# A graph network's edge strips: preparing edges in six steps, one-hots a group ahead, one multiplication for three

## The chip, the cores and the metric

The kernel runs on one core of a Trainium2 chip. Its engines are TensorE (PE; its weight loads are listed as PEld), VectorE (DVE), ScalarE (ACT), GpSimd (POOL) and the queue that issues most transfers (SP). The metric is the device time of one launch in microseconds, median of several runs. Times within the profiled execution are counted from the start of its span.

## The reference

Four graph layers over 6250 nodes with 128 features and 206250 edges, sorted by target `dst`. Each layer works on `h = relu(layernorm(x))` and is added to `x`:

```python
# layer 0: weighted sum over the edges, two products
neighbor = segment_sum(edge_weight[:, None] * h[src], dst)
x += leaky_relu(neighbor @ W1.T + b1 + (h * neighbor) @ W2.T + b2, 0.2)
# layer 1: mean over the edges, gelu, a norm over all nodes
agg = segment_sum(h[src], dst) / max(deg, 1)
f = gelu(agg @ Wl.T + bl + h @ Wr.T);  x += graph_norm(f) + h
# layer 2: mean of the cliques' rows at the other end
x += mean(x_clique[dst], by=src) @ W.T + b
# layer 3: a gated unit on the summed messages
x += gru(segment_sum((h @ W_in.T + b_in) @ W_msg, dst), ...) @ W_out.T + b_out
```

## The kernel before

The kernel does not gather rows. It turns the edges into dense matrices: for each block of 128 target nodes, how often each source node occurs (`cnt`, kept in device memory for layers 1 to 3) and the sum of its edge weights (`edge_w`, used at once by layer 0). The 6250 nodes are 49 blocks; a **strip** is two blocks, 256 target nodes, and there are 25 strips (the last has one block). All of this is done in the first part of `fast`, up to line 829; behind it `dense` (line 838) reads the matrices back for layers 1 to 3, and that part is not touched.

A strip goes through these hands:

- `prepare(k)` finds the edges of every target node. DVE counts in a sample of `dst` (`junk`, line 628) where a node's edges begin; POOL fetches a `line` of 128 edges there (635, by an indirect transfer, the helper `fetch` at line 620); DVE counts within it (`less`, `c`, `off`). For each of two halves POOL then fetches 64 entries of `dst` (655); DVE marks those of the node (`same`, 657), moves `off` on by their number and marks the others (661); POOL fetches `src` and the weights. DVE splits `src` into a block and a place in it (666 to 670, `vals` 1 and 0), POOL splits the weight into three parts (672, `vals` 2 to 4). PE transposes the five (676) and ACT copies them to `by_edge` (678). Its working tiles have one buffer each (`once`), `vals` and `by_edge` two.
- `count` takes 32 target nodes at a time, a **group**; a strip has eight. For a group DVE makes the one-hots: `s_hot` (696) and `k_hot`, first the block alone (698), then times each of the three weight parts (700). PE multiplies them in 96 small matmuls, 24 to each of four tiles `pK` (713), and ACT copies each `pK` to `cnt` (727) and `edge_w` (728). The one-hots have two buffers, `pK` three, `cnt` two. After four groups a `cnt` is complete: SP writes it to `cnt_d` (736), and for the first 25 blocks turns it in seven pieces (741, `tt` with three buffers) and stores these too (742).
- `layer0(k)` runs one strip later, a step of six products `pL` (749) behind each group, then the copy `agg` (754), a transpose (757) and `inter` (759).
- `finish0` runs one strip later still, in three steps: the products with W1 and W2 (768, 769), bias and leaky relu (`full`), the norm of the result (`norm`, called at 779: statistics on DVE, `f_std` on ACT at 558, `f_rstd` and `f_shift` on DVE, the relu on ACT at 565), stores of `u_d` and `h_d`; then the transposes of `h1` (786); then the product with Wr (793), `fs` (795) and its store.
- `norms` makes `h0` from `x` in the first strips.

The source interleaves them by generators: after each group of `count` one step of the layer before and one of its end is asked for. `prepare` of the next strip is asked for whole at the strip's beginning, except for the transposes, which are asked for after group 4. A scheduler takes this order as a priority only: it places each instruction on its engine when its inputs and a free buffer are there by its own reckoning, so an engine's sequence can differ from the source's. Once placed, each engine works its sequence in order.

Of the kernel before, what the change touches and what calls it, by code (L numbers as in the profile page):

```python
# [16 lines left out]
P = 128  # L17
# [468 lines left out]
def fast(ctx: ExitStack, tc: tile.TileContext, a: dict, out: bass.AP, flag: bass.AP):  # L486
# [62 lines left out]
    def norm(xs, hs, nb):  # L549
# [3 lines left out]
        for j in range(nb):  # L553
# [27 lines left out]
    with ExitStack() as bx:  # L581
# [22 lines left out]
        def norms():  # L604

            for g, nb in GROUPS:
                xs = xpool.tile([P, GB, D], F32, name="xs")
                load_x(xs, g, nb)
                norm(xs, h0[:, g : g + nb, :], nb)
                if g // GB % 2:  # L610
                    yield
# [11 lines left out]
        def prepare(k):  # L623
# [11 lines left out]
            fetch(line, "dst", at_i)  # L635
            less = once.tile([P, P], BF16, name="less")
# [12 lines left out]
            for h in range(WN):  # L649
# [5 lines left out]
                fetch(dst[:, half], "dst", off_i)  # L655
                here = deg[:, k, h : h + 1]
# [7 lines left out]
                fetch(wgt[:, half], "edge_weight", off_i)  # L664
            sb = once.tile([P, P], I32, name="sb")
# [15 lines left out]
        def count(k, nb, by_edge, edge_w):  # L681


            mats = []
            for t0 in range(0, nb * P // WN, TW):
                tq = TW // TI

                def at(i, n):
                    v = by_edge[:, i, t0 : t0 + TW].rearrange("p (q o t) -> p q o t", o=1, t=TI)
                    return v.to_broadcast([P, tq, n, TI])  # L690

                def count_up(n):
                    return iota[:, None, :n, :].to_broadcast([P, tq, n, TI])

                s_hot = hot.tile([P, tq, P, TI], BF16, name="s_hot")
                nc.vector.tensor_tensor(s_hot, count_up(P), at(0, P), op=ALU.is_equal)  # L696
                k_hot = hot.tile([P, 4, tq, NB, TI], BF16, name="k_hot")
                nc.vector.tensor_tensor(k_hot[:, 0], count_up(NB), at(1, NB), op=ALU.is_equal)  # L698
                for i in range(1, 4):
                    nc.vector.tensor_tensor(k_hot[:, i], k_hot[:, 0], at(1 + i, NB), op=ALU.mult)  # L700
                for q in range(0, TW, PW):

                    pk = psum.tile([P, WN, 512], F32, name="pK", bufs=3)
                    for i in range(PW):
                        (u, t), o = divmod(q + i, TI), 2 * NB * i
                        for j in (0, 2, 3):
                            for h in range(WN):
                                r = slice(h * H, (h + 1) * H)
                                if j:
                                    to, rhs = slice(o + NB, o + 2 * NB), k_hot[r, j, u, :, t]  # L710
                                else:
                                    to, rhs = slice(o, o + 2 * NB), k_hot[r, :2, u, :, t]
                                nc.tensor.matmul(pk[:, h, to], s_hot[r, u, :, t], rhs, start=j == 0,  # L713
                                                 stop=True, skip_group_check=True)
                    n0 = (t0 + q) * WN
                    nn = PW * WN
                    if n0 % P == 0:
                        mats.append(cnts.tile([P, NB, P], BF16, name="cnt"))

                    def by_block(half):  # L720
                        v = pk[:, :, : 2 * PW * NB].rearrange("p h (i c b) -> p c b i h", c=2, b=NB)
                        return v[:, half]

                    def to_nodes(m):
                        return m.rearrange("p b (i h) -> p b i h", h=WN)

                    nc.scalar.copy(to_nodes(mats[n0 // P][:, :, n0 % P : n0 % P + nn]), by_block(0))  # L727
                    nc.scalar.copy(to_nodes(edge_w[:, :, n0 : n0 + nn]), by_block(1))  # L728
                yield
                n0 = (t0 + TW) * WN  # L730
                if n0 % P:
                    continue
                j = n0 // P - 1
                g = k * SB + j
                c, i = CHUNK_OF[g]
                nc.sync.dma_start(cnt_d[c, :, i, :], flat(mats[j]))
                if g >= NQB:
                    continue
                for q in range(0, NB, 7):
                    tt = turned.tile([P, 7, P], BF16, name="tt")  # L740
# [79 lines left out]
        for _ in ends.pop():  # L820
            pass
# [315 lines left out]
```

## Time and profile before

| what | value |
| --- | --- |
| median of 3 runs | 2179.38 us (2178.58 to 2182.17) |
| the profiled execution | 2177.09 us, span 2175.3 us, 60376 instructions |
| TensorE clock granted, mean | 0.962 |
| first matmul of the strips (L713) | at 53.0 us |
| strips 0 to 24 | 53.0 to about 1224 us |
| dense layers behind them | about 1224 to 2175 us |
| DVE one-hots L696, L698, L700 | 239.3, 114.4 and 307.9 us busy, for 196 groups |
| PE L713 and L749 | 420.8 and 590.0 us busy |
| ACT L727 and L728 | 407.5 and 415.1 us busy |

The busy times of PE are modelled and overlap, so they are read with the distances between groups in the timeline. A line number names the line of the kernel that issued an instruction; where a helper issues it, it is the helper's (POOL's fetches are all L620, and are told apart by their tiles). The bracket behind an instruction in the timeline is the idle time of its engine just before it and what ended it.

### The profile page before, as it was taken

The numbers are of one execution on the slowest core, as the hardware profiler recorded it, in microseconds if no ns is written. First come the engines' busy times: TensorE is split into PE (matmuls) and PEld (weight loads), VectorE is DVE, ScalarE is ACT, GpSimd is POOL, SyncE is SP. The second block draws the span as 40 slices with busy tenths as digits, with TensorE's granted clock in tenths as the row PEclk, the third lists the DMA queues.
The fourth block names the chain that finished last, engine by engine and source line by source line (L and its number), as shares of the span: only waits on it lengthen the run. The fifth ranks groups of instructions, "written<-read, shape, count | busy, mean of one in ns | idle before, by whom it ended". The sixth has DMA issues, their size and how long they took to land. (4 is left out here: it accounts for less than half of the span.)

```text
span 2175.3 us, 60376 instructions
## 1 busy us (share of the span) xinstructions
PE 1910.5 (88%) x25624; PEld 1564.8 (72%) x25624; DVE 1411.9 (65%) x3349; ACT 1174.2 (54%) x2692; POOL 348.3 (16%) x377
## 2 busy tenths in 40 slices
PE   0579988889898999998999679999878899999998
PEld 0557777777787888777888558878756667777775
DVE  6887767767676776776775458677776554443443
ACT  1745656555555666566666146566545555443443
POOL 4531211222212122111100020000231110000000
PEclk9989999999999999999999789999989999999999
DMA  2579999999998222223122698688755778776773
GB/s 63 154 177 229 216 213 212 231 204 217 220 229 194 86 105 93 90 85 105 73 101 103 197 265 278 214 283 270 228 164 174 231 236 262 239 229 197 237 239 128
DMA packets 423787, 406.32 MB, mean 187 GB/s; under 512 B 191216, under 2 KB 414307, under 8 KB 417235
## 3 DMA queue, kind: packets, MB, share of 16 engines
q1 hardware_dynamic: 414883, 394.35, 64.1%
q0 software_dynamic: 5600, 6.56, 1.3%
q8 instruction: 203, 3.33, 0.6%
q10 hardware_dynamic: 3024, 1.45, 0.3%
q14 instruction: 77, 0.63, 0.1%
HBM read 227.26 MB, written 134.89 MB: 166 GB/s over the span
## 5 line engine op out<-in xcount | busy, mean ns | idle before, releaser
L727 ACT CAST cnt<-pK 128x392 bf16<-128x392 f32 x784 | 407.5, 520 | 342.1 <-PE pK L713 289.5
L749 PE MATMUL pL<-edge_w,h 128*128 128x256 f32 (+1 forms) x2450 | 590.0, 392 | 1.1 <-issue 0.8
L713 PE MATMUL pK<-k_hot,s_hot 64*128 64x49 bf16 (+1 forms) x18816 | 420.8, 195 | 126.4 <-ACT edge_w L728 66.0
L713 PEld LDWEIGHTS <-s_hot 64*128 64x128 bf16 x18816 | 371.0, 96 | 197.2 <-issue 119.8
L749 PEld LDWEIGHTS pL<-edge_w,h 128*128 128x128 f32 x2450 | 456.9, 196 | 66.2 <-issue 1.2
L728 ACT COPY edge_w<-pK 128x392 f32<-128x392 f32 x784 | 415.1, 529 | 0.0
L870 PE MATMUL acc<-some,parts 128*128 128x512 f32 (+1 forms) x1456 | 369.4, 395 | 31.3 <-DVE some L865 20.6
L870 PEld LDWEIGHTS acc<-some,parts 128*128 128x128 f32 x1456 | 269.6, 192 | 95.7 <-DVE some L865 24.4
L696 DVE TENSOR_TENSOR s_hot<-iota,by_edge 128x2048 bf16<-128x2048 bf16 x196 | 239.3, 1221 | 133.7 <-PE pK L713 129.2
L700 DVE TENSOR_TENSOR k_hot<-k_hot,by_edge 128x784 bf16<-128x784 bf16 x588 | 307.9, 576 | 5.2
L859 ACT CAST others<-ring 128x1536 fp32r<-128x1536 bf16 (+3 forms) x156 | 192.4, 1233 | 198.3 <-PE acc L870 132.2
L858 DVE CAST some<-ring 128x2048 fp32r<-128x2048 bf16 (+3 forms) x156 | 165.7, 1063 | 177.8 <-PE acc L870 151.6
L870 PE MATMUL acc<-others,parts 128*128 128x512 f32 (+1 forms) x1092 | 277.7, 388 | 0.0
L865 DVE TENSOR_SCALAR_CACHE_REDUCE some<-ring 128x512 fp32r<-128x512 bf16 (+1 forms) x364 | 216.6, 651 | 62.7 <-PE acc L870 43.1
L870 PEld LDWEIGHTS acc<-others,parts 128*128 128x128 f32 x1092 | 202.5, 191 | 42.5 <-issue 0.5
L868 ACT ACTIVATE others<-ring 128x512 fp32r<-128x512 bf16 (+1 forms) x273 | 162.3, 597 | 113.1 <-issue 59.6
L870 PE MATMUL acc<-some,q_parts 128*128 128x512 f32 (+1 forms) x390 | 111.5, 412 | 30.6 <-DVE some L858 30.6
L698 DVE TENSOR_TENSOR k_hot<-iota,by_edge 128x784 bf16<-128x784 bf16 x196 | 114.4, 583 | 0.0
L870 PEld LDWEIGHTS acc<-some,q_parts 128*128 128x128 f32 x390 | 71.2, 196 | 51.4 <-DVE some L858 35.5
L657 DVE TENSOR_SCALAR_CACHE_REDUCE same<-dst,node 128x64 bf16<-128x64 int32 x50 | 13.9, 277 | 137.7 <-DMA dst<-in_dst,off_i 137.7
L780 POOL TENSOR_TENSOR xs<-xs,h 128x256 f32<-128x256 f32 (+1 forms) x25 | 27.3, 1090 | 466.3 <-ACT h L565 466.3
L870 PE MATMUL acc<-others,q_parts 128*128 128x512 f32 (+1 forms) x260 | 78.3, 409 | 0.0
(155 smaller groups left out, 1520.6 us busy)
## 6 DMA issues: line engine op xcount, KB each, us to landing
ring<-cnt_d SPq DMA_DIRECT2D x168, 896.0 KB
cnt_d<-cnt SPq DMA_DIRECT2D x49, 1568.0 KB
cntT_d<-tt SPq DMA_DIRECT2D x175, 224.0 KB
ring<-cntT_d SPq DMA_DIRECT2D x60, 640.0 KB
ring<-cnt_d SPq DMA_DIRECT2D x14, 224.0 KB
xs<-in_x SPq DMA_DIRECT2D x24, 128.0 KB
xs<-in_x SPq DMA_DIRECT2D x12, 256.0 KB
h_d<-h SPq DMA_DIRECT2D x24, 128.0 KB
```

Source lines behind the costliest of these rows:

```text
L696: nc.vector.tensor_tensor(s_hot, count_up(P), at(0, P), op=ALU.is_equal)
L698: nc.vector.tensor_tensor(k_hot[:, 0], count_up(NB), at(1, NB), op=ALU.is_equal)
L700: nc.vector.tensor_tensor(k_hot[:, i], k_hot[:, 0], at(1 + i, NB), op=ALU.mult)
L713: nc.tensor.matmul(pk[:, h, to], s_hot[r, u, :, t], rhs, start=j == 0, stop=True, skip_group_check=True)
L727: nc.scalar.copy(to_nodes(mats[n0 // P][:, :, n0 % P : n0 % P + nn]), by_block(0))
L728: nc.scalar.copy(to_nodes(edge_w[:, :, n0 : n0 + nn]), by_block(1))
L749: nc.tensor.matmul(pl[:, :w], h0[:, s, :], edge_w[:, s, :w], start=s == 0, stop=s == NB - 1)
L858: nc.vector.tensor_copy(some[:, :dve, :nb], t[:, :dve])
L859: nc.scalar.copy(others[:, : step - dve, :nb], t[:, dve:])
L865: nc.vector.tensor_scalar(rhs, t[:, i], 1.0, None, op0=ALU.mult, op1=ALU.add, accum_out=total)
L868: nc.scalar.activation(rhs, t[:, i], AF.Copy, accum_out=total)
L870: nc.tensor.matmul(acc[:, :w], parts[:, q + i, j, :], rhs, start=q + i + j == 0, stop=q + i + j == last)
```

## The change

Five things. `prepare` gets yields after the fetch of `line`, after each fetch of `dst`, after the last fetches and after the weights' split, and its transposes are the sixth step; the main loop asks for one step behind each group. The one-hots become a function of their own, `one_hots`, called for the next group (or the next strip's first) before `count` is called for this one. `norm` gets three yields, so `finish0` has six steps, and the loop asks for it before the layer's step instead of after. `by_edge` becomes two tiles in another order of axes, copied by two instructions, so that one multiplication writes all three weighted parts of `k_hot`. The stores of a finished `cnt` are a function `store`, called at the same place.

```diff
@@ norm
         nc.vector.tensor_scalar(std[:, :nb], mv[:, :nb, 1], EPS, None, op0=ALU.add)
+        yield
         nc.scalar.activation(std[:, :nb], std[:, :nb], AF.Sqrt)
+        yield
 ...
         nc.vector.scalar_tensor_tensor(shift[:, :nb], mv[:, :nb, 0], -1.0, rstd[:, :nb],
                                        op0=ALU.mult, op1=ALU.mult)
+        yield
@@ prepare
             fetch(line, "dst", at_i)
+            yield
 ...
                 fetch(dst[:, half], "dst", off_i)
+                yield
 ...
                 fetch(wgt[:, half], "edge_weight", off_i)
+            yield
 ...
-            by_edge = pay.tile([P, 5, P], BF16, name="by_edge")
-            nc.scalar.copy(by_edge, pv)
+            keys = pay.tile([P, P // TI, 2, TI], BF16, name="keys")
+            parts = pay.tile([P, P // TI, 3, TI], BF16, name="by_edge")
+            for t, i in ((keys, 0), (parts, 2)):
+                to = pv[:, i : i + t.shape[2], :].rearrange("p i (q t) -> p q i t", t=TI)
+                nc.scalar.copy(t, to)
+            by_edge = keys, parts
             yield by_edge
@@ count, now one_hots and count
+        def one_hots(by_edge, t0):
+            of = slice(t0 // TI, t0 // TI + tq)
+            keys, parts = (t[:, of, :, None, :] for t in by_edge)
 ...
+            s_hot = hot.tile([P, tq, P, TI], BF16, name="s_hot")
+            nc.vector.tensor_tensor(s_hot, count_up(P), at(0, P), op=ALU.is_equal)
-                k_hot = hot.tile([P, 4, tq, NB, TI], BF16, name="k_hot")
-                nc.vector.tensor_tensor(k_hot[:, 0], count_up(NB), at(1, NB), op=ALU.is_equal)
-                for i in range(1, 4):
-                    nc.vector.tensor_tensor(k_hot[:, i], k_hot[:, 0], at(1 + i, NB), op=ALU.mult)
+            k_hot = hot.tile([P, tq, 4, NB, TI], BF16, name="k_hot")
+            nc.vector.tensor_tensor(k_hot[:, :, 0], count_up(NB), at(1, NB), op=ALU.is_equal)
+            nc.vector.tensor_tensor(k_hot[:, :, 1:], k_hot[:, :, :1].to_broadcast([P, tq, 3, NB, TI]),
+                                    parts.to_broadcast([P, tq, 3, NB, TI]), op=ALU.mult)
+            return s_hot, k_hot
+        def count(t0, hots, mats, edge_w):
+            s_hot, k_hot = hots
 ...
+        def store(g, mat):
 ...
@@ finish0
-            norm(xs, h1, nb)
+            yield from norm(xs, h1, nb)
@@ the main loop
-        edges, before, ends = prepare(0), norms(), []
-        next(edges)
-        by_edge = next(edges)
+        for by_edge in prepare(0):
+            pass
+        before, ends, hots = norms(), [], one_hots(by_edge, 0)
         for k, nb in STRIPS:
             edges = prepare(k + 1) if k + 1 < NS else iter(())
-            next(edges, None)
             edge_w = edge.tile([P, NB, SW], F32, name="edge_w")
-            end = ends.pop() if ends else iter(())
-            turned_edges = None
-            for i, _ in enumerate(count(k, nb, by_edge, edge_w)):
-                next(before, None)
-                next(end, None)
-                if i == 4:
-                    turned_edges = next(edges, None)
-            by_edge = turned_edges
+            end, mats, following = ends.pop() if ends else iter(()), [], None
+            for t0 in range(0, nb * P // WN, TW):
+                now, t1 = hots, t0 + TW
+                if t1 * WN < nb * P:
+                    hots = one_hots(by_edge, t1)
+                elif following:
+                    hots = one_hots(following, 0)
+                count(t0, now, mats, edge_w)
+                next(end, None)
+                next(before, None)
+                following = next(edges, None) or following
+                if t1 * WN % P == 0:
+                    store(k * SB + len(mats) - 1, mats[-1])
+            by_edge = following
             for _ in chain(before, end):
                 pass
             before = layer0(k, nb, edge_w)
-        for _ in chain(ends.pop(), before):
-            pass
-        for _ in ends.pop():
-            pass
+        end = ends.pop()
+        for _ in before:
+            next(end, None)
+        for _ in chain(end, ends.pop()):
+            pass
```

The other two callers of `norm` run through its steps at once.

More of the change, by code (lines that the diff above doesn't have):

```diff
@@ L608, in norms @@
                 load_x(xs, g, nb)
-                norm(xs, h0[:, g : g + nb, :], nb)
+                for _ in norm(xs, h0[:, g : g + nb, :], nb):
+                    pass
                 if g // GB % 2:
@@ L676, in prepare @@
                 nc.tensor.transpose(pv[:, i, :], vals[:, i, :], identh)
-            by_edge = pay.tile([P, 5, P], BF16, name="by_edge")
-            nc.scalar.copy(by_edge, pv)
-            yield by_edge
[L681 to L696, printed above, removed]
-                k_hot = hot.tile([P, 4, tq, NB, TI], BF16, name="k_hot")
-                nc.vector.tensor_tensor(k_hot[:, 0], count_up(NB), at(1, NB), op=ALU.is_equal)
-                for i in range(1, 4):
[L700 to L740, printed above, removed]
-                    nc.sync.dma_start_transpose(tt, flat(mats[j][:, q : q + 7, :]))
-                    nc.sync.dma_start(cntT_d[:, g, q * P : (q + 7) * P], flat(tt))
@@ new lines, in prepare, with at, count_up @@
+            keys = pay.tile([P, P // TI, 2, TI], BF16, name="keys")
[4 more added lines that the diff above has]
+            by_edge = keys, parts
+            yield by_edge
+        tq = TW // TI
+        def one_hots(by_edge, t0):
+            of = slice(t0 // TI, t0 // TI + tq)
+            keys, parts = (t[:, of, :, None, :] for t in by_edge)
+            def at(i, n):
+                return keys[:, :, i].to_broadcast([P, tq, n, TI])
+            def count_up(n):
+                return iota[:, None, :n, :].to_broadcast([P, tq, n, TI])
+            s_hot = hot.tile([P, tq, P, TI], BF16, name="s_hot")
[5 more added lines that the diff above has]
+            return s_hot, k_hot
@@ new lines, in count, with by_block, to_nodes @@
+        def count(t0, hots, mats, edge_w):
+            s_hot, k_hot = hots
+            for q in range(0, TW, PW):
+                pk = psum.tile([P, WN, 512], F32, name="pK", bufs=3)
+                for i in range(PW):
+                    (u, t), o = divmod(q + i, TI), 2 * NB * i
+                    for j in (0, 2, 3):
+                        for h in range(WN):
+                            r = slice(h * H, (h + 1) * H)
+                            if j:
+                                to, rhs = slice(o + NB, o + 2 * NB), k_hot[r, u, j, :, t]
+                            else:
+                                to, rhs = slice(o, o + 2 * NB), k_hot[r, u, :2, :, t]
+                            nc.tensor.matmul(pk[:, h, to], s_hot[r, u, :, t], rhs, start=j == 0,
+                                             stop=True, skip_group_check=True)
+                n0 = (t0 + q) * WN
+                nn = PW * WN
+                if n0 % P == 0:
+                    mats.append(cnts.tile([P, NB, P], BF16, name="cnt"))
+                def by_block(half):
+                    v = pk[:, :, : 2 * PW * NB].rearrange("p h (i c b) -> p c b i h", c=2, b=NB)
+                    return v[:, half]
+                def to_nodes(m):
+                    return m.rearrange("p b (i h) -> p b i h", h=WN)
+                nc.scalar.copy(to_nodes(mats[n0 // P][:, :, n0 % P : n0 % P + nn]), by_block(0))
+                nc.scalar.copy(to_nodes(edge_w[:, :, n0 : n0 + nn]), by_block(1))
@@ L744, in layer0 @@
+        def store(g, mat):
+            c, i = CHUNK_OF[g]
+            nc.sync.dma_start(cnt_d[c, :, i, :], flat(mat))
+            for q in range(0, NB if g < NQB else 0, 7):
+                tt = turned.tile([P, 7, P], BF16, name="tt")
+                nc.sync.dma_start_transpose(tt, flat(mat[:, q : q + 7, :]))
+                nc.sync.dma_start(cntT_d[:, g, q * P : (q + 7) * P], flat(tt))
         def layer0(k, nb, edge_w):
@@ L1015, in fast @@
         h = work.tile([P, CB, D], F32, name="wb")
-        norm(xg, h, nb)
+        for _ in norm(xg, h, nb):
+            pass
         nc.gpsimd.tensor_tensor(xg, xg, bcast(b_out, nb), op=ALU.add)
```

## The prediction

> **What bounds the kernel now.** I read the page's engine shares and slices first, then the busy time by stretches, then the timeline of TensorE (PE), VectorE (DVE) and GpSimd (POOL) around one strip's end, last the waits of the DMA queue. The change touches only the first 1224 us, the strips; the dense part behind them keeps its code.
>
> ```profile
> PE 1910.5 (88%) x25624; PEld 1564.8 (72%) x25624; DVE 1411.9 (65%) x3349; ACT 1174.2 (54%) x2692; POOL 348.3 (16%) x377
> 211.90:782.90 571.00, 510.65 (x10646) 436.66 (x10646) 401.97 (x889) 334.68 (x840) 123.33 (x143) 0.95 0.85 200
> 782.90:1048.90 266.00, 244.85 (x5324) 209.73 (x5326) 191.95 (x401) 167.39 (x421) 52.23 (x62) 1.00 0.27 91
> 1048.90:1173.30 124.40, 120.25 (x2664) 104.09 (x2665) 88.58 (x158) 83.57 (x211) 4.93 (x7) 1.00 0.24 93
> ```
>
> The three stretches (columns: length, busy PE, PEld, DVE, ACT, POOL, then clock, DMA share, GB/s) are strips 3 to 14, 15 to 20 and 21 to 23; a strip begins at the first L713 matmul of its eight groups. The last three strips take 41.5 us each with PE 97% busy: that is PE's own time. In strip 22 the starts of the groups lie 5.79, 5.06, 5.34, 4.84, 5.18, 4.92, 4.85 and 5.50 us apart; the bare group is 4.84, the rest are the small products placed in it. Strips 15 to 20 take 44.3, strips 3 to 14 47.6, so 2.8 and 6.1 us a strip are waits, and they sit at the strip's end:
>
> ```profile
> 901.15 0.79 DVE L698 TENSOR_TENSOR k_hot<-iota,by_edge 128x784 bf16<-128x784 bf16 x1
> 906.25 0.28 DVE L657 TENSOR_SCALAR_CACHE_REDUCE same<-dst,node 128x64 bf16<-128x64 int32 x1 [4.32 <-DMA dst<-in_dst,off_i]
> 906.46 1.51 DVE L700 TENSOR_TENSOR k_hot<-k_hot,by_edge 128x784 bf16<-128x784 bf16 x3
> 911.81 0.28 DVE L657 TENSOR_SCALAR_CACHE_REDUCE same<-dst,node 128x64 bf16<-128x64 int32 x1 [3.52 <-DMA dst<-in_dst,off_i]
> 918.35 0.41 DVE L759 TENSOR_TENSOR inter<-agg,pD 128x256 f32<-128x256 f32 x1
> ...
> 903.08 0.95 POOL L620 DMA_INDIRECT dst<-in_dst,off_i  x1 [0.30 <-issue]
> 908.50 0.94 POOL L620 DMA_INDIRECT dst<-in_dst,off_i  x1 [3.23 <-DVE off_i L652]
> ...
> 914.37 0.22 PE L713 MATMUL pK<-k_hot,s_hot 64*128 64x98 bf16 x2 [0.86 <-DVE k_hot L700]
> 917.34 2.86 PE L749 MATMUL pL<-edge_w,h 128*128 128x256 f32 x12
> 920.03 0.38 PE L768 MATMUL pD<-f_W1T,agg 128*128 128x128 f32 x2
> ```
>
> Read it as one chain. The transposes L676 of a strip's edges end at 897.83 (call this T). POOL then splits the weights and issues the next fetch of dst 5.25 us later; DVE, already done with the one-hots, stands for it in line (first `same` at T+8.4), stands again for the second fetch (issued 2.25 us after the first `same`), and only then makes the one-hots of group 0. PE loses 0.86 + 0.25 + 0.28 us there, which is little because DVE was a group ahead. `inter` (L759) comes after two more sets of one-hots, at 918.76, and PE asks for it at 920.03, with the six steps of pL (L749) in front.
>
> **The order of the changed kernel.** Its instructions as built show how little is spread. DVE's sequence at the strip's end, POOL's whole sequence and nearly all of SP's are those of before; tiles come free as before, and that, not the place in the source, holds the edges' steps back. What does move: (a) the transposes of the edges stand behind group 5 instead of 4, so T and the whole chain behind it come one group later against the strip's end: the first `same` now stands in the one-hots of group 0, the second behind them, `less` in those of group 1, and `inter` directly behind these. (b) On PE the end of layer 0 is issued ahead of pL: in each group 0 the products with W1 and W2 (L768, L769) stand before the six steps of pL, and they wait for `inter`. (c) h1's transposes and the product with Wr go from groups 1 and 2 to 4 and 5. So everything that PE has left in group 0 now queues behind an operation which DVE reaches only after two fetches of dst.
>
> **Part by part.**
> Strips 15 to 20. From T, nominal: group 6 4.84, group 7 5.49 (its L757 and seventh step are in it), matmuls of group 0 2.2 (897.77 to the free buffer at 900.01): PE reaches the product with W1 at T+12.5. DVE: first `same` at T+8.1 (mean of the seven fetches from 722 to 987; 7.7 to 8.5), multiplication done by T+9.8, just before PE's group 0 at T+10.3; second fetch issued 2.15 after the first `same` (2.25 less the saved 0.14 below), landed 3.2 later (2.8 to 3.6): T+13.4. Then 0.2, s_hot 1.15, k_hot 0.59, multiplication 1.4, `inter` 0.41: T+17.2. PE stands 4.7 us. The 2.8 us of before go: DVE has then caught up, and ScalarE no longer holds a copy back for `f_std`.
> Strips 3 to 14 also wait for `line`. First `same` T+9.0, multiplication T+10.6 (0.3 late); second `same` T+14.5; s_hot and k_hot T+16.4; the fetch of line goes out 2.5 after the second dst and lands 3.6 later (4.30 at 445.62), so `less` at T+17.3, multiplication T+18.9, c and `inter` T+19.55. PE stands 0.3 + 6.75.
> The clock. In strip 1 PE stood 4.73 us for one-hots, and the rows after it run at half clock:
>
> ```profile
> 141.22 0.26 PE L713 MATMUL pK<-k_hot,s_hot 64*128 64x98 bf16 x2 [4.73 <-DVE k_hot L700]
> 144.81 3.69 PE L749 MATMUL pL<-edge_w,h 128*128 128x256 f32 x12
> 139.70:143.10 3.40, 1.41 (x39) 1.16 (x41) 2.56 (x10) 0.17 (x1) 0.51 (x1) 0.50 0.95 276
> 143.10:146.50 3.40, 3.40 (x70) 3.06 (x64) 2.23 (x5) 3.05 (x8) 0.43 (x1) 0.50 0.90 142
> ```
>
> Twelve L749 take 3.69 instead of 2.86 and the 92 L713 ahead of them 2.70 instead of 1.9: 1.6 us lost. I take 1.6 at each of the 18 strip beginnings; bounds 0 (the waits of 0.86 at 914 left the clock at 1.00) and 2.4.
> [...]
>
> [...]
> Sums. 15 to 20: 41.5 + 4.7 + 1.6 = 47.8, six of them 286.8 for 266.0: +20.8. 3 to 14: 41.5 + 0.3 + 6.75 + 1.6 = 50.15, twelve 601.8 for 571.0: +30.8.
> SP. From 212 to 695 us SP is never long idle, and what it waits for is its own transfers:
>
> ```profile
> SPq L742 <- DMA tt<-cnt: 93.3, 88, 3.3
> SPq L736 <- ACT edge_w L728: 4.8, 9, 1.4
> ```
>
> So the queue alone needs about (483 - 7) / 10 = 47.6 us a strip while counts are turned. Below that strips 2 to 12 cannot fall whatever DVE does; at 50.15 the queue is covered, so I add nothing for it. Its issues are the same in number; u_d's store moves ahead of the last store of a turned piece, f_d's ahead of a turning; both sources are ready (f_d waited 0.5 us in ten strips).
> One multiplication for three. Rows L696 (2048 elements, 1221 ns) and L700 (784, 576) give 0.176 us + 0.51 ns each: 2352 elements 1.38 us. Three in a row take 1.51, since they overlap: 0.14 saved a group, 27 us of DVE in all, beside PE except the two in the chain, counted above. If the wider pattern ran at the rate of the f32 rows (L1061: 512 in 661 ns, L777: 256 in 420), it would be 2.4 us: the upper bound.
> Edges copied in two: 128x640 took 697 ns; two copies by the rows L754 (256, 368) and L1040 (512, 560) about 0.85: ScalarE +0.15 a strip, under POOL's 5.25 us; 0 to +4 in all. The end of layer 0 in steps: the same instructions. `fs` (L795) now stands between s_hot and k_hot of group 7, but its products are done 0.6 us after the matmuls of group 5 while s_hot takes 1.15: 0. `f_std` stands two copies into group 1, 6.1 us after `inter` by PE's clock (3.4 of products, 1.3 of half clock, 1.4 of group 1), and DVE is there after 5.4: 0; were it late, ScalarE would hold PE by 0.7 as in group 2 of strips 15 to 19 now (6.04 for 5.34). In strips 21 to 24 no fetch is left and `inter` comes about 1.4 us before PE asks: 0.
> Start: the first pK stood at 53.0 because the multiplications of group 0 waited behind a `same`, `vals` and `src` of the next strip (49.87 to 51.5); now they follow the one-hots at once: -3 (0 to -6). Strips 0 to 2, 159 us, are crowded with norms; their order is reshuffled both ways: 0, bounds -5 and +6.
> Total: 20.8 + 30.8 - 3 = +48.6. The profiled execution took 2177.1 (span 2175.3 and 1.8 around it), so 2225.7; the median shown is 2.3 above it: 2228, given as 2227.
>
> **Rivals.**
> The wait is hidden (faster). If the second dst landed 4.7 us sooner, or DVE were a whole group further ahead, `inter` would be in time. Then 15 to 20 keep at most their 2.8 (-17), 3 to 12 fall from 48.2 to SP's 47.6 at best (-6), 13 and 14 to 41.5 (-6), start -3: 2147. For it: less work on DVE. Against it: every fetch of 18 took at least 2.4 us from issue to use, and two follow each other. It decides once `inter` ends before T+12.5. 7%.
> No change: the scheduler had spread the steps already, so it moves nothing: 2179. For it: POOL's order; against it: (b), plain in PE's order. 4%.
> The multiplication falls to the slow rate: +1.0 us of DVE a group, 8 a strip on top; DVE would need about 8 x 4.2 + 9 of other work + 9 of standing = 52 a strip, some 4 above the forecast's strips at 25 strips: 2320. Against it: L696 and L700 repeat pairs in the same manner. 4%.
>
> **How the numbers follow.** The forecast has 85%. Its own ends: low, the fetches at their shortest (standing 4.0 and 5.9), no loss of clock and the start's bounds: +7 + 1 - 11, 2176 by the median; high, 5.5 and 8 with 2.4 of clock, +4 for the copies, +6 for the first strips: +30 + 55 + 10, 2274. Eight in ten: 2190 to 2262. What this kernel's measurement tells from no change is about 0.2%, 4 us. Faster 0.08, same 0.03, slower 0.89.
>
> **What would show it.** Right: in strips 3 to 20 the first matmul with W1 in group 0 has 4 to 7 us of idle time ended by DVE `inter`; pL behind it; half clock in the window after; strips of about 48 and 50 us; strips 21 to 23 still 41.5; first pK near 50; the single multiplication near 1.38 us. Wrong: no idle time there, strips at 44 or below, or a multiplication over 2 us.

## The result, and the profile after

The changed kernel takes 2286.71 us (median of four runs, 2282.90 to 2296.31) against 2178.98 for the kernel before: a ratio of 1.0494, 95% interval 1.0470 to 1.0519. It is slower, as forecast, by 108 us where the forecast had 49, and above its range of 2190 to 2262. The profiled execution took 2285.36 us, its span is 2283.6, the granted clock 0.928 on the mean (0.962 before).

The page's engine shares, then the busy time by stretches (length, busy PE, PEld, DVE, ACT, POOL, clock, DMA share, GB/s) for strips 3 to 14, 15 to 20 and 21 to 23:

```profile
PE 1915.3 (84%) x25624; PEld 1566.6 (69%) x25624; DVE 1372.1 (60%) x2957; ACT 1173.9 (51%) x2717; POOL 348.6 (15%) x377
```

```profile
209.10:858.20 649.10, 513.72 (x10647) 438.06 (x10648) 385.76 (x701) 334.52 (x853) 125.00 (x144) 0.89 0.71 177
858.20:1163.00 304.80, 256.21 (x5323) 218.65 (x5322) 182.50 (x305) 167.23 (x427) 54.69 (x64) 0.90 0.24 80
1163.00:1287.80 124.80, 120.75 (x2662) 103.40 (x2662) 83.18 (x110) 83.61 (x214) 4.89 (x7) 1.00 0.24 93
```

DVE has 40 us less to do than before, and in the last three strips PE is 97% busy as it was (41.6 us a strip). The time is lost earlier. Strips 3 to 14 take 649.1 us instead of 571.0 (+78.1) and strips 15 to 20 304.8 instead of 266.0 (+38.8). The rest is small: the first pK stands at 51.8 (-1.2), strips 0 to 2 take 1.6 less, strips 21 to 23 0.4 more, everything from strip 24 on 6.2 less. A second profile of the same kernel had 1003 us for that last part, against 1002 before and 996 here, so the 6.2 is scatter. The sum is +108.3.

Nearly all of the loss sits in group 0 of each strip. The waits of PE (who waits for whom, total, times, longest) of the kernel after, then the same strip as shown before (strip 17; timelines of DVE, POOL, SP and PE):

```profile
PE pD L778 <- DVE inter L769: 148.8, 19, 11.1
PE pK L728 <- ACT edge_w L743: 40.2, 93, 3.6
PE pK L728 <- DVE k_hot L709: 30.5, 10, 5.5
PE pK L728 <- issue: 4.1, 9, 1.1
```

```profile
958.02 0.28 DVE L663 TENSOR_SCALAR_CACHE_REDUCE same<-dst,node 128x64 bf16<-128x64 int32 x1 [4.07 <-DMA dst<-in_dst,off_i]
958.23 1.38 DVE L709 TENSOR_TENSOR k_hot<-k_hot,by_edge 128x2352 bf16<-128x2352 bf16 x1
965.93 0.28 DVE L663 TENSOR_SCALAR_CACHE_REDUCE same<-dst,node 128x64 bf16<-128x64 int32 x1 [5.87 <-DMA dst<-in_dst,off_i]
969.17 0.41 DVE L769 TENSOR_TENSOR inter<-agg,pD 128x256 f32<-128x256 f32 x1
...
960.13 0.94 POOL L624 DMA_INDIRECT dst<-in_dst,off_i  x1 [2.85 <-DVE off_i L657]
...
958.14 0.33 SPq L748 DMA_DIRECT2D cnt_d<-cnt  x1
...
961.78 0.58 PE L728 MATMUL pK<-k_hot,s_hot 64*128 64x98 bf16 x24 [0.20 <-ACT edge_w L743]
969.64 0.79 PE L778 MATMUL pD<-f_W1T,agg 128*128 128x128 f32 x2 [7.27 <-DVE inter L769]
971.50 4.41 PE L759 MATMUL pL<-edge_w,h 128*128 128x256 f32 x12
```

This is the chain of the forecast, row by row: the first `same` 8.3 us after the edges' transposes (949.7), the second fetch of dst 2.1 later, the product with W1 waiting for `inter` and pL behind it. Two rows differ. The second fetch, issued at 960.13, is not used until 965.93, 5.8 us later instead of 3.2; a store of 1.6 MB went out 2 us ahead of it, at 958.14. And pL runs at 4.41 us for twelve instead of 2.86 over its whole length; the clock (third number from the right in the rows below, by windows of 3.4 us) is halved from the gap itself on, for three windows:

```profile
961.20:964.60 3.40, 0.97 (x48) 0.77 (x40) 0.00 (x0) 2.87 (x8) 0.95 (x1) 1.00 0.54 201
964.60:968.00 3.40, 0.00 (x0) 0.00 (x0) 2.03 (x5) 0.00 (x0) 0.00 (x0) 0.50 0.01 1
968.00:971.40 3.40, 1.76 (x8) 1.76 (x9) 2.72 (x3) 0.00 (x0) 0.00 (x0) 0.50 0.00 0
971.40:974.80 3.40, 3.40 (x10) 2.77 (x10) 3.02 (x6) 0.00 (x0) 0.00 (x0) 0.50 0.00 0
974.80:978.20 3.40, 3.26 (x102) 2.68 (x102) 1.23 (x8) 1.73 (x6) 0.00 (x0) 0.99 0.02 5
```

Read from the start times of the matmuls, group 0 falls into three parts (us, means over the strips named; the sum of the three is the group):

| kernel, strips | pK first to last | last pK to W1 | W1 to group 1 | whole strip |
| --- | --- | --- | --- | --- |
| after, 3 to 10 | 2.91 | 9.00 | 6.18 | 54.24 |
| after, 15 to 20 | 2.02 | 6.87 | 6.11 | 50.81 |
| after, 21 to 23 (no wait) | 2.00 | 0.12 | 3.68 | 41.59 |

So a strip of 15 to 20 is 41.6, plus 6.75 of standing, plus 2.4 of clock; the forecast had 4.7 and 1.6. The other seven groups of a strip take nearly what they take undisturbed. In strips 3 to 10 and in 12 it is `less` that comes late; in strips 11 and 13 it is the second `same`, 8.3 and 6.8 us after its fetch. In strip 7 (POOL, SP, DVE and PE) line is fetched at 431.01, and SP issues the store at 430.98.

```profile
431.01 0.95 POOL L624 DMA_INDIRECT line<-in_dst,at_i  x1 [0.31 <-DVE at_i L637]
...
430.98 0.43 SPq L748 DMA_DIRECT2D cnt_d<-cnt  x1
...
437.74 0.29 DVE L642 TENSOR_SCALAR less<-line,f_node 128x128 bf16<-128x128 int32 x1 [4.84 <-DMA line<-in_dst,at_i]
439.90 0.80 PE L778 MATMUL pD<-f_W1T,agg 128*128 128x128 f32 x2 [7.53 <-DVE inter L769]
```

The expectations below speak of five theories. 1: the loss comes from DVE standing for two fetches of dst in a row, which makes `inter` late, with PE queued behind it. 2, its rival: the order on PE alone made the loss. 3: the second dst and line land late because the 1.6 MB store of the strip's second cnt is on its way. 4: certain waits of PE that the profile can't explain belong to the chip and hour of a run and not to an edit. 5: the halved clock behind a long wait is a cost of its own.

Three questions were open: whether the two reorderings (the edges a group later, W1 ahead of pL) are the cause and in what shares; why the fetches land late; and whether the halved clock is a cost of its own. The ratios below are to the kernel before on the same chip, since its median lay between 2174 and 2186 us from one set of runs to the next.

### The profile page after: what moved, and what is told of

Same layout as the page of the kernel before. It is cut to its first block, busy times and chain, and to the rows that moved or that the text cites. A ratio compares the mean times of both kernels' runs of the same rounds, so it can differ in the third digit from the quotient of the medians.

```text
span 2283.6 us, 60035 instructions
## 1 busy us (share of the span) xinstructions
PE 1915.3 (84%) x25624; PEld 1566.6 (69%) x25624; DVE 1372.1 (60%) x2957; ACT 1173.9 (51%) x2717; POOL 348.6 (15%) x377
## 5 line engine op out<-in xcount | busy, mean ns | idle before, releaser
L759 PE MATMUL pL<-edge_w,h 128*128 128x256 f32 (+1 forms) x2450 | 597.1, 397 | 0.3 <-ACT agg L764 0.3
L759 PEld LDWEIGHTS pL<-edge_w,h 128*128 128x128 f32 x2450 | 469.0, 201 | 66.7 <-ACT agg L764 0.5
L728 PE MATMUL pK<-k_hot,s_hot 64*128 64x49 bf16 (+1 forms) x18816 | 403.9, 194 | 89.0 <-ACT edge_w L743 40.2
L728 PEld LDWEIGHTS <-s_hot 64*128 64x128 bf16 x18816 | 362.4, 96 | 163.2 <-issue 125.8
L706 DVE TENSOR_TENSOR s_hot<-iota,keys 128x2048 bf16<-128x2048 bf16 x196 | 240.4, 1226 | 202.3 <-PE pK L728 196.4
L709 DVE TENSOR_TENSOR k_hot<-k_hot,by_edge 128x2352 bf16<-128x2352 bf16 x196 | 270.7, 1381 | 4.7
L778 PE MATMUL pD<-f_W1T,agg 128*128 128x128 f32 x98 | 31.5, 419 | 148.9 <-DVE inter L769 148.8
L778 PEld LDWEIGHTS pD<-f_W1T,agg 128*128 128x128 f32 x98 | 22.8, 287 | 151.5 <-DVE inter L769 151.2
L708 DVE TENSOR_TENSOR k_hot<-iota,keys 128x784 bf16<-128x784 bf16 x196 | 113.6, 580 | 0.0
L663 DVE TENSOR_SCALAR_CACHE_REDUCE same<-dst,node 128x64 bf16<-128x64 int32 x50 | 13.9, 278 | 151.0 <-DMA dst<-in_dst,off_i 150.9
```

The source lines that it names most:

```text
L708: nc.vector.tensor_tensor(k_hot[:, :, 0], count_up(NB), at(1, NB), op=ALU.is_equal)
L709: nc.vector.tensor_tensor(k_hot[:, :, 1:], k_hot[:, :, :1].to_broadcast([P, tq, 3, NB, TI]), parts.to_broadcast([P, tq, 3, NB, TI]), op=AL ...
L759: nc.tensor.matmul(pl[:, :w], h0[:, s, :], edge_w[:, s, :w], start=s == 0, stop=s == NB - 1)
```

## The experiments

### The two reorderings, one at a time and both

First, W1 and W2 go back behind pL:

```diff
-                next(end, None)
                 next(before, None)
+                next(end, None)
```

> Only the order of layer 0's step and its end is turned back (pL ahead of the products with W1 and W2 in group 0); the edges' transposes stay behind group 5. Theory 1 (`inter` comes late because DVE stands for two dst fetches in a row, and PE queues behind it): the lateness stays, PE only has the six products pL, 2.86 us, in front of the wait. Wait of the first product with W1 about 3.9 us in strips 15 to 20 (6.0 to 7.3 in the changed kernel) and about 6.2 in strips 3 to 13 (7.5 to 11.1); 18 x 2.9 = 52 us saved: 2235 us, down to 2217 if each strip loses 1 us less to the halved clock. Theory 2 (the order on PE alone made the loss): back to about 2180.

Measured: 2237.36 us, ratio 1.0212 (1.0173 to 1.0251). From the last pK to W1 it is 4.7 to 5.8 us in strips 15 to 19, of which the six steps of pL fill 2.8; so PE stands about 2 us where 3.9 were expected, because the last pK itself comes later after the edges' transposes (14.4 to 15.9 us for 12.5). The idle time ended by `inter` falls from 148.8 to 37.2 us in all:

```profile
PE pD L778 <- DVE inter L769: 37.2, 17, 4.0
```

Theory 1 holds, and the total is close to the 2235 us expected: more than half of the loss goes and a ratio of 1.02 stays, so the order on PE alone is not the cause.

Second, the edges go back and W1 stays ahead:

```diff
         for k, nb in STRIPS:
             edges = prepare(k + 1) if k + 1 < NS else iter(())
+            for _ in range(5):
+                next(edges, None)
...
-                following = next(edges, None) or following
+                if t0 == 4 * TW:
+                    following = next(edges, None)
```

> Only the edges' steps are put back: five steps are asked for at the strip's beginning, the transposes behind group 4; the end of layer 0 stays ahead of pL. Theory 1: the chain of fetches lies one group earlier against the strip's end, `inter` comes 1.0 to 1.6 us after PE asks for it in strips 15 to 20; no row in strips 3 to 13 waits over 3 us; 2180 to 2200 us. The second dst then lands some 3.2 us and line some 3.6 us after issue, as in the kernel before. Theory 2 (order on PE alone): most of the 108 us stays, 2240 or more.

Measured: 2183.09 us, ratio 0.9975 (0.9956 to 0.9994). The whole loss is gone, and W1 ahead of pL costs next to nothing where `inter` is in time: in strips 15 to 20 PE waits at most 0.4 us for it, not the 1.0 to 1.6 expected:

```profile
PE pD L778 <- DVE inter L769: 0.9, 3, 0.4
```

The second `same` comes 2.3 to 2.9 us after the issue of its fetch in strips 14 to 19 and `less` 2.6 to 3.9 after line's in strips 3 to 13 (2.8 to 3.6 and 3.0 to 4.3 in the kernel before). DVE still stands for dst (101.7 us in all); what differs is where in the strip it does.

Third, both go back, which leaves the one multiplication, the six steps of the end and the one-hots ahead (the two edits together).

> Both orders are turned back (edges as before, pL ahead of W1 and W2); what is left of the change is the single multiplication, the one-hots asked for a group ahead, the end of layer 0 in six steps and the first strip's order. Theory 1: these cost nothing: the kernel before less the 1.2 us of the start and up to 3 x 0.14 us in each of 18 strips: 2165 to 2180 us. Rival (they cost something of their own, for example f_std holding a copy or h1's products in groups 4 and 5): over 2185 us, with a wait in a group other than 0.

Measured: 2183.43 us, ratio 0.9987 (0.9969 to 1.0004). The median lies above the 2165 to 2180 expected, but the kernel before ran at 2186 in the same set. The other parts together do no harm that this can tell, and no visible good.

The two effects are far from additive: +2.1% for the edges a group later alone, nothing for W1 ahead alone, +5% together. The edges' place makes `inter` late, the order on PE decides how much work PE can still do while it is late.

### The three small parts

The multiplication alone, in the kernel before (the two tiles that it reads come with it):

```diff
-                for i in range(1, 4):
-                    nc.vector.tensor_tensor(k_hot[:, i], k_hot[:, 0], at(1 + i, NB), op=ALU.mult)
+                nc.vector.tensor_tensor(k_hot[:, :, 1:], k_hot[:, :, :1].to_broadcast([P, tq, 3, NB, TI]),
+                                        parts.to_broadcast([P, tq, 3, NB, TI]), op=ALU.mult)
```

> The kernel before with one part of the change alone: keys and parts as two tiles, one multiplication of 2352 elements for three of 784. The order on every engine is that of the kernel before. 1.38 us for 1.51: up to 3 x 0.14 us less in each of the 18 strips where DVE is late, 0 to 7 us: ratio 0.997 to 1.000. Rival (the wider pattern or the second copy costs): over 1.002.

Measured: 2167.39 us, ratio 0.9964 (0.9948 to 0.9980). It is the one part of the change that was seen to gain by itself, about 8 us, which is what 0.14 us in each of three groups of 18 strips come to.

The end of layer 0 in three steps again:

```diff
-            yield from norm(xs, h1, nb)
+            for _ in norm(xs, h1, nb):
+                pass
```

> The changed kernel with layer 0's end in three steps again (the norm in one), so that h1's transposes and the product with Wr stand in groups 1 and 2 as before; all else as changed. If the six steps cost and save nothing: within 6 us of the changed kernel, ratio to it 0.997 to 1.003. If f_std in group 1 or the transposes behind it hold PE: up to 0.7 us in each of 18 strips slower, 13 us, seen as a longer group 1 or 2.

Measured: 2295.39 us, ratio 1.0565 (1.0525 to 1.0605); the changed kernel in the same set 1.0526 (1.0493 to 1.0558). No difference that these can tell. In strips 15 to 17 groups 1 and 2 take 1.07 us more (5.48 and 5.31 for 4.85 and 4.87) and groups 4 and 5 0.62 less, and group 0 gives back the rest (14.9 for 15.3): strips of 51.2 for 51.1. The steps move the small products about and that is all.

The changed kernel a second time, in that same set:

> The changed kernel itself, a second time. In the four runs before this one PE waited 45 to 59 us for nothing that the profile shows (issue) in front of pK, in the profiles of the two kernels only 4 us. Theory 4 (that belongs to the chip and the hour of those runs, not to what was edited): it is there in this run too, 40 us or more, and the ratio to the kernel before stays at 1.047 to 1.052, or falls by up to 0.01 because the time lies inside waits. Rival (it comes with the edits): 4 us again, ratio 1.047 to 1.052.

Measured: 2288.86 us, ratio 1.0526. PE waits 5.1 us for issue. The other kernels of this set (the multiplication 4.7, the end in three steps 6.2) show none of it either, while all four kernels of the set before had 45 to 59 us, about half to three quarters of it in groups 6 and 7, some 0.45 us at a time. As far as these sets show, it goes with the set of runs and not with an edit, so the half of theory 4 that puts it down to the chip and the hour stands (the sets of these experiments each ran on another chip, so the two can't be told apart); that it would be there in this run was wrong. What it is stays open.

### Why the fetches land late

In strips 12 to 22 the store of the second cnt is held back by a real dependency (it cannot go out before group 2 of the next strip is copied):

```diff
+                if late and t0 == 2 * TW:
+                    g, mat = late.pop()
+                    zero = small.tile([P, 1], F32, name="zero")
+                    nc.scalar.activation(zero, edge_w[:, 0, t0 * WN : t0 * WN + 1], AF.Relu, scale=0.0)
+                    nc.scalar.activation(mat[:, 0, :1], mat[:, 0, :1], AF.Relu, bias=zero)
+                    store(g, mat)
...
+                    if g >= NQB and t1 * WN == SW and k + 2 < NS:
+                        late.append((g, mats[-1]))
```

> The changed kernel, but for strips 12 to 23 the 1.6 MB store of a strip's second cnt is held back until group 2 of the next strip is copied (two small operations on ScalarE make it wait). Theory 3 (the second dst fetch, issued some 10.4 us after the edges' transposes, lands late because that store, issued at 8.4, is on its way): in strips 14 to 20 second `same` comes 3.2 us after the issue (3.9 to 5.8 in the changed kernel), PE stands about 4.7 to 5.2 us instead of 6.0 to 7.3; seven strips by 2.0 us, with some clock: 2268 to 2274 us; strips 3 to 11 as in the changed kernel. Rival (such a fetch takes that long there in any case): waits as they were, 2283 to 2290 us.

Measured: 2259.69 us, ratio 1.0279 (1.0212 to 1.0345; three of the four runs lie at 2258.79 to 2261.82, one at 2233.01). In strip 17 of this kernel (timelines of DVE, POOL, SP, PE) the fetch lands 2.4 us after its issue:

```profile
947.56 0.28 DVE L663 TENSOR_SCALAR_CACHE_REDUCE same<-dst,node 128x64 bf16<-128x64 int32 x1 [2.44 <-DMA dst<-in_dst,off_i]
...
945.19 0.94 POOL L624 DMA_INDIRECT dst<-in_dst,off_i  x1 [3.04 <-DVE off_i L657]
...
964.81 5.33 SPq L748 DMA_DIRECT2D cnt_d<-cnt  x2
...
951.27 0.49 PE L778 MATMUL pD<-f_W1T,agg 128*128 128x128 f32 x2 [1.69 <-DVE inter L769]
```

Over strips 14 to 20 the second `same` comes 2.3 to 2.9 us after the issue. In both profiles of the changed kernel it comes after 4.4 to 5.8 us in strips 14 to 19, and after 3.8 and 3.9 us in strip 20, where the store goes out only once the fetch has landed. Theory 3 is right, and the effect is a little larger than the 2.0 us that was expected, 2.5 on the mean. PE stands 1.7 to 2.5 us there, partly because group 7 was 1.7 us longer in this set by waits for issue, which delay PE and not DVE; the time of the strip, which has these waits in it, is the fairer number, 47.4 for 50.8 in strips 15 to 20. The total came out 8 us below the expected range.

In strips 3 to 11 the same store can be moved with one line, behind the turning:

```diff
-            nc.sync.dma_start(cnt_d[c, :, i, :], flat(mat))
             for q in range(0, NB if g < NQB else 0, 7):
                 tt = turned.tile([P, 7, P], BF16, name="tt")
                 nc.sync.dma_start_transpose(tt, flat(mat[:, q : q + 7, :]))
                 nc.sync.dma_start(cntT_d[:, g, q * P : (q + 7) * P], flat(tt))
+            nc.sync.dma_start(cnt_d[c, :, i, :], flat(mat))
```

> The changed kernel with one line moved: a finished cnt is first turned and then written to cnt_d, so in strips 3 to 11 the 1.6 MB store goes out behind the first three turnings, some 5 us later. Theory 3 carried over to these strips (line is issued in the same microsecond as this store, 431.0 in strip 7, and lands late for it): `less` comes 3.6 to 5 us after the issue of line instead of 6.6 to 8.1, PE stands 5.5 to 7.5 us in strips 3 to 11 instead of 7.5 to 11, 10 to 30 us saved, ratio to the changed kernel 0.987 to 0.996. Rival (the turnings, not the store, keep the small fetch back): line as late as before, same time within 6 us. Strips 13 to 20 unchanged in both.

Measured: 2248.58 us, ratio 1.0301 (1.0256 to 1.0346), 0.979 to 0.982 of the changed kernel by that kernel's two ratios: some 40 to 50 us saved, more than the 10 to 30 expected. Strip 7 of this kernel (POOL, SP, DVE, PE):

```profile
412.11 0.94 POOL L624 DMA_INDIRECT line<-in_dst,at_i  x1 [0.31 <-DVE at_i L637]
...
412.16 4.02 SPq L750 DMA_TRANSPOSE tt<-cnt  x3
416.23 0.58 SPq L752 DMA_DIRECT2D cnt_d<-cnt  x1
...
416.85 0.28 DVE L642 TENSOR_SCALAR less<-line,f_node 128x128 bf16<-128x128 int32 x1 [2.80 <-DMA line<-in_dst,at_i]
...
419.00 0.80 PE L778 MATMUL pD<-f_W1T,agg 128*128 128x128 f32 x2 [5.54 <-DVE inter L769]
```

`less` comes 3.0 to 4.7 us after line's issue in strips 3 to 11 (6.5 to 8.1 in the two profiles of the changed kernel), PE stands 4.8 us on the mean instead of 9.0, and strips 3 to 10 take 50.04 us instead of 54.24. The turning of three pieces, which is on its way instead, does not hold the fetch back; the store does. Strips 15 to 20, where nothing is turned, stay as they were (51.1). The landing gains 3.9 us on the mean of strips 3 to 10 and pK ends half a microsecond later, which is about the 4.2 us of the wait. That second `same` and `less` both come sooner in strips 11 to 13 (50.3 us for 54.6) is of the same kind.

### The clock

Extra products ahead of W1, which need nothing from DVE, keep PE busy while it would stand. (pL is overwritten by its first real product, so the result is untouched.)

```diff
             pl = psum.tile([P, SW], F32, name="pL")
+            for _ in range(24):
+                nc.tensor.matmul(pl[:, :w], h0[:, 0, :], edge_w[:, 0, :w], start=True, stop=True)
+            yield
             for s in range(NB):
...
+                if not t0:
+                    next(before, None)
                 next(end, None)
                 next(before, None)
```

> The changed kernel with 24 extra products in front of W1 in each group 0 (the first step of pL, done over and over into pL before it is begun; 24 x 0.238 = 5.7 us of work that needs nothing from DVE). They fit inside the 6.0 to 11.1 us in which PE stands. Theory 5 (the halved clock behind each long wait is a cost of its own): the twelve pL of group 0 take 2.9 us again instead of 4.4; each of 18 strips gains what the clock cost: 2.8 to 3.4 us by the rows of the changed kernel, so 2225 to 2240 us; by the 1.6 us of the forecast, 2258. The wait itself, by the time from the edges' transposes to W1, stays. Rival (the clock costs nothing, since DVE or ScalarE hold the end of group 0 anyway): 2283 to 2292.

Measured: 2382.50 us, ratio 1.0904 (1.0860 to 1.0949). The expectation had the size of its own filler wrong: each product stands in the trace as two matmuls (48 rows for 24), and together they took 10.5 us, longer than the wait. The time is thus no answer, but one row is: from W1 to group 1 it took 3.58 to 3.68 us in strips 3 to 23, against 6.1 to 6.2 in the changed kernel. The next run fits the filler to the wait (against the run before):

```diff
-            for _ in range(24):
+            for _ in range(15):
```

> The changed kernel with 15 extra products in front of W1 in each group 0. In the run with 24 they were two passes each and took 10.4 us, so W1 came 3.9 us later in strips 15 to 20 than it had to wait, but from W1 to group 1 it then took 3.58 us instead of 6.1. 15 take 6.5 us and fit inside the wait of 6.7 us in strips 15 to 20 and of 9 us in strips 3 to 13. Theory 5 (2.5 us of each strip is the halved clock, lost on top of the wait): strips 15 to 20 at 48.3 us instead of 50.8, W1 to group 1 3.6 us; strips 3 to 13, where 2.5 us of the wait stay empty, between 51.5 (clock full) and 54.2 (halved all the same); strips 21 to 23, which have no wait, 6.5 us longer each: 2243 to 2285 us in all, the parts by strip decide. Rival (the 24 products changed something else): strips 15 to 20 stay at 50.5 or more.

Measured: 2344.94 us, ratio 1.0719 (1.0674 to 1.0763), well above the expected range. By strips, as the expectation asked: in strips 16 to 20 W1 still comes 6.7 us after the last pK, and W1 to group 1 takes 3.58 us; in strip 17 the clock stays at 1.00 (timeline of PE and ScalarE, then the windows with the clock):

```profile
982.27 6.74 PE L759 MATMUL pL<-edge_w,h 128*128 128x256 f32 x30
988.85 0.38 PE L781 MATMUL pD<-f_W1T,agg 128*128 128x128 f32 x2
989.74 2.76 PE L762 MATMUL pL<-edge_w,h 128*128 128x256 f32 x12
995.26 0.58 PE L728 MATMUL pK<-k_hot,s_hot 64*128 64x98 bf16 x24 [1.42 <-ACT edge_w L743]
...
992.89 0.20 ACT L559 ACTIVATE f_std<-f_std 128x2 f32<-128x2 f32 x1 [8.85 <-DVE f_std L557]
```

```profile
982.20:985.60 3.40, 3.40 (x24) 2.98 (x18) 1.68 (x4) 1.84 (x5) 0.00 (x0) 1.00 0.28 105
985.60:989.00 3.40, 3.40 (x18) 3.00 (x17) 3.37 (x5) 0.00 (x0) 0.00 (x0) 1.00 0.00 0
989.00:992.40 3.40, 3.40 (x21) 2.83 (x19) 3.21 (x8) 0.00 (x0) 0.00 (x0) 1.00 0.00 0
```

Group 0 falls from 15.0 to 12.55 us: the halved clock is 2.5 us of each strip on top of the wait, as theory 5 says. But the strip does not fall to 48.3, it takes 51.6. Group 1 takes back 0.7 us in most strips and more in some (5.55 to 10.0 us instead of 4.85), because ScalarE now stands for `f_std` and the norm's relu ahead of the copies that PE needs (1.42 us at 995.26); and this run again had the waits for issue (55.1 us in all, group 7 longer by 1.7 us), as the four kernels of the first set did. Part of what the clock costs is thus covered by something that would come late anyway, and filling the gap with idle work is no remedy: strips 21 to 23, which have no gap, take 48.7 us for 41.5.

The trace also shows how much PE worked beside a halved clock. It has the clock in steps of 3.41 us; the rows of strip 17 above have 0.97 us of PE's work in one at full clock, then 0.00, 1.76 and 3.40 in three halved ones, then the full clock again. In strips 3 to 22 of the changed kernel, 18 steps at full clock are followed by a halved one, and PE worked 0.0 to 1.7 us in each of these; in those followed by another full one it worked 2.0 us or more. In the halved steps that another follows it worked 0.0 to 2.7 us, in those that the full clock follows 2.9 or more. These are counts in one trace, and no limit is read from them: in the kernel before a step with 1.67 us (from 399.13) is followed by the full clock and one with 1.74 us (from 498.12) by a halved one. The length of one gap does not tell it either: in the run that holds the store back PE stands only 1.7 to 2.5 us in strips 15 to 20, and their mean clock is 0.96, about one halved step in each, with 5.2 to 5.4 us from W1 to group 1, 1.6 us lost.

### Steps that are really spread

The change asks for the edges' steps one behind each group, but as built they are hardly spread. The prediction put that down to when tiles come free, which no run tests. Here they are held by a dependency: `less` and each `same` get their scalar through two tiny operations that read the newest one-hots.

```diff
+        def held(v):
+            # v once the newest one-hots are made
+            if not ahead:
+                return v
+            none = small.tile([P, 1], F32, name="none")
+            nc.vector.tensor_scalar(none, ahead[-1][:, 0, 3, 0, :1], 0.0, None, op0=ALU.mult)
+            w = small.tile([P, 1], F32, name="held")
+            nc.vector.tensor_add(w, none, v)
+            return w
...
-            nc.vector.tensor_scalar(less, line, n0, None, op0=ALU.is_lt)
+            nc.vector.tensor_scalar(less, line, held(n0), None, op0=ALU.is_lt)
...
                 yield
+                node = held(node)
                 here = deg[:, k, h : h + 1]
...
+            ahead.append(k_hot)
             return s_hot, k_hot
```

With pL ahead of W1 (the edit of the first experiment added):

> The changed kernel with pL ahead of W1 and W2, and with the steps of the edges really spread: `less` and each `same` take their scalar through two tiny operations that read the newest one-hots, so DVE cannot come to them before these are made, a group or more after the fetch was issued. Theory 1 (what costs is DVE standing for fetches inside the one-hots): no wait of DVE for dst over 1 us, strips 15 to 20 at 41.5 to 42.5 us (44.3 in the kernel before), plus up to 2 us of issue; strips 3 to 12 stay at the 47.6 us that SP needs for the turning; 2150 to 2165 us, ratio 0.985 to 0.995. Rival (another wait takes its place, or the extra operations cost what they save): 0.998 or more.

Measured: 2137.68 us, ratio 0.9822 (0.9792 to 0.9851), faster than both kernels and better than expected. The waits of DVE for dst in the changed kernel, then those for src and dst in this one:

```profile
DVE same L663 <- DMA dst<-in_dst,off_i: 150.9, 43, 7.6
...
DVE sb L686 <- DMA src<-in_src,off_i: 96.2, 24, 5.8
DVE same L676 <- DMA dst<-in_dst,off_i: 5.7, 3, 2.0
```

The 150.9 us of DVE standing for dst are 5.7, and in strip 17 `inter` is made at 840.48, and PE comes to W1 at 844.94. DVE still stands once in each strip, for src (3.26 us at 860), but with a group of one-hots in hand. Strips 15 to 20 take 43.0 us, half a microsecond more than expected without waits for issue; groups 2 and 6 of strips 15 to 17 take 5.9 us for 4.9 and 5.0. And most of the gain against the kernel before is not where it was expected. In the profiled execution strips 15 to 20 gain 7.9 us, strips 3 to 14 (47.3 us each, near what SP needs) 3.8, while the first matmul comes 7.2 us earlier and strips 0 to 2 gain 18.6; strips 21 to 23 lose 8.4, most of it in the last one. Why the first strips gain is not shown.

With W1 ahead of pL, as the change has it:

> The changed kernel as it is, W1 and W2 ahead of pL, but with the spread steps of the edges (`less` and each `same` held until the newest one-hots are made). Theory 1 (W1 ahead costs only when `inter` is late): no wait for `inter` over 1 us, strips 15 to 20 at 41.5 to 42.5 us, 2125 to 2140 us, as fast as the same with pL ahead or up to 10 us faster, since the transposes of the edges then do not stand inside the matmuls of group 6. Rival (W1 ahead costs by itself): 2150 us or more, with the wait for `inter` over 2 us.

Measured: 2140.89 us, ratio 0.9815 (0.9780 to 0.9849), just past the upper end of what was expected and the same as with pL ahead. `inter` is in time, and then the order on PE is free. It confirms the two runs at the top from the other side.

## Why the prediction went wrong in size

**The chain and its place: right.** T (the end of the edges' transposes) one group later; first `same` at T+7.8 to 9.0 (10.5 in strip 13); the second issue 2.1 us behind it (3.6 in strip 11); W1 ahead of pL; `inter` directly behind the one-hots of group 1; PE standing in strips 3 to 20 and not in 21 to 24, where strips stayed at 41.6. The runs with one reordering undone confirm both (a) and (b), and that they work together.

**"Landed 3.2 later" and "lands 3.6 later": the steps that failed.** Both durations came from the trace of before, where the chain lay one group earlier. The prediction moved the chain by a group and kept the landing times. At its new place they go out beside the 1.6 MB store that follows the last group: the second dst of strips 14 to 19 some 2.0 to 2.6 us behind it, line in strips 3 to 10 from the same moment to 1.8 us behind it. They are used after 4.4 to 5.8 and 6.5 to 8.1 us. PE stood 6.75 us for the 4.7 forecast in strips 15 to 20 and 9.0 for 6.75 in strips 3 to 14, some 40 us of the 60 that were missing. That the store makes them land late, the two runs that move only the store show: 2.3 to 2.9 and 3.0 to 4.7 us. With it moved, strips 15 to 20 take 47.4 us and strips 3 to 10 50.04, for 47.8 and 50.15 in the forecast. That this comes out so close is partly luck: in strips 3 to 10 of that run PE stands 4.6 us where 6.75 were forecast, its matmuls of group 0 are 1.4 us late where 0.3 were, and the clock costs 2.3 where 1.6 were. The prediction had named the wait it would cost, and had not asked what else is on its way at that moment.

**"1.6 at each of the 18 strip beginnings": too small.** It was read at a gap of 4.73 us, where the clock was halved for 6.8 us, 1.5 of them in the gap. At gaps of 6.4 to 11.1 us the trace shows 10.2 to 13.7 us of half clock, the first part of it in the gap (6.8 in strip 20, at a gap of 6.0); 2.5 us were lost on the mean, at the outside of the bounds given (2.4). 0.9 times 18 is 16 us. The one reading did not carry over to longer gaps: strip 1 of the kernel before had two halved steps of 3.41 us, these have three or four, and two in strip 20. Nor did shorter ones leave the clock at 1.00: waits of 1.7 to 2.5 us still went with a halved step (above), and in the kernel before two gaps of 1.57 and 1.60 us, ended at 402.15 and 406.01, with a clock of 0.51 from 405.9 to 409.3.

**Terms that held.** The multiplication: 1.381 us measured for 1.38. SP: not the limit in strips 3 to 14 at 54 us (ScalarE waits 6.8 us in all for a turned piece, 21.0 before). The end in six steps: nothing. `f_std`: nothing in the changed kernel, though with a full clock (the runs with extra products) it is the next thing that is late, by the 0.7 us named. The start: -1.2 instead of -3. Strips 0 to 2: -1.6 for 0. The range's upper end was set from 5.5 and 8 us of standing with 2.4 of clock, 2274, and cut to 2262; the standing was 6.75 and 9.

**The rivals.** None came about. Hidden waits are what the held steps bring, so that rival had the right mechanism for another kernel.

## What to carry to other kernels

When a chain of small fetches is moved against the rest of the kernel, look up which large transfers are on their way at its new place before its landing times are carried over; here one 1.6 MB store about doubled them. An engine that works in order should not come to a fetched operand before it must: where the order as built has it come there too early, a cheap dependency that holds the consuming instruction back a group does what a place in the source did not do. And a wait of PE is to be priced with the clock on top: here some 2.5 us behind waits of 6 to 11 us, and still 1.6 behind waits of 1.7 to 2.5.

## What was not expected of the hardware

- A fetch of 64 entries per partition is used 2.3 to 3.6 us after its issue in strips 14 to 19, where nothing is turned, when no store of cnt is near it, and after 4.4 to 5.8 us with a 1.6 MB store issued 2.0 to 2.6 us earlier; a fetch of line after 3.0 to 4.7 us beside turnings and 6.5 to 8.1 us beside the store.
- In strips 3 to 19 of the changed kernel, gaps of 6.4 to 11.1 us on PE went with a clock halved for 10.2 to 13.7 us, part of it in the gap; in strip 17 of the run with 15 extra products, which kept PE busy in the gap, it stayed at 1.00. With waits of only 1.7 to 2.5 us, in strips 15 to 20 of the run that holds the store back, the mean clock was 0.96.
- In two of the four sets of experiments PE waited 45 to 59 us in front of pK for nothing that the profile shows, in steps of some 0.45 us, mostly three to five in a strip (four kernels in one set, one in the other); in the other two sets, and in the first profiles of the two kernels, 1 to 7 us. Its cause is open.
